# Sorted attention: the first group of 512 tokens in two halves of 256, with the second group's gathers moved behind both

## Chip, cores and metric

The kernel runs on one core of one Trainium2 chip. The metric is device time in microseconds (us), the median of several executions. A profile is one further execution with the hardware profiler on; times "at 1345" are us from the start of its span.

## What is computed

A block of two layers on 16 x 256 tokens of width 512, all in float32. The part that matters here is the second attention, after a mixture of experts:

```python
x = x + _L0_ffn_ref(_layernorm(x), ...)             # experts and shared network
x = x + _L1_xattn_ref(_layernorm(x), ctx, seg_id)   # the attention below
x = x + _L1_ffn_ref(_layernorm(x), ...)
...
q_c = q @ W_dq                                      # 512 -> 192
q_nope = q_c @ W_uq                                 # 16 heads of 128
q_rope = _rope(q_c @ W_qr)                          # 16 heads of 64
scores = (q_nope . k_nope + q_rope . k_rope) * scale
good = (k_ids <= seg) & (k_ids >= seg - 8)          # at most nine keys for a query
attn = softmax(where(good, scores, -1e30))
out = (attn @ v) @ W_o
```

## The kernel before

The program is laid out in stages: convolution with the shared network, experts (`routed`), the attention over sorted tokens (`attention_sorted`), the last network (`ffn`). An instruction scheduler places the instructions of each engine in a fixed order when the program is built, roughly in the order in which the code asks for them; every engine then works through its own queue in order. `tc.issue_after(i)` makes the instructions under it stand behind instruction `i`.

In `attention_sorted` the 4096 tokens have been sorted by the key they look at. They are worked on in 32 tiles of 128 tokens (`T`), four tiles to a group (`g`, 512 tokens, `T4 = 4`, `N = 512`). For a group:

- `fetch(T)` gathers, by indirect DMAs that GpSimd issues (line 1870), a tile's rows of x (`xt`) and its rope rows (`rr`); `fetch_routed` gathers, in two such DMAs, the experts' rows (`ygd`) that belong to it, into four buffers `g_yt`. `fetch_keys(T)` gathers a tile's windows of keys in four (`gw`). The x and rope rows of tiles 0 to 3 and the keys of tiles 0 to 2 are fetched in the stage before.
- `tokens` adds the gated experts' rows on VectorE (L1440), normalizes (`layernorm`: statistics L66 and L68 on VectorE, L70 and L71 on GpSimd, L72 on VectorE), and turns rope rows (L1448) and tokens (L99) on TensorE. `self.normed` is the last L71.
- `latents` makes q_c of the whole group (L1458, L1469).
- `heads(st, two)` makes four heads' queries for the whole group, and is called four times: matmuls L1482, L1485, L1489, L1493 into six of seven PSUM slots; ScalarE copies a swapped half (L1498), VectorE multiplies with the cosine (L1500), GpSimd with the sine (L1501) and adds (L1502); ScalarE stores the other queries (L1506). Results go to the big buffers `qn` and `qr`.
- For each tile `window` turns the keys (L1515, L1520) and makes masks, `scores` (L1543, L1549) needs the tile's part of `qn` and `qr`, `weigh` and `weights` are the softmax on VectorE and ScalarE, `values` is L1589, and `project` (L1605, 32 passes) adds to `xt` (L1610) and stores it.

The main loop (`for T in range(NT_ + 2)`) runs scores of tile T, values of T - 1, projection of T - 2, and puts the next group's fetches, `tokens`, `latents` and `heads` between them. Before the loop, group 0 goes through `tokens`, `latents` and `heads` with nothing else to do. The names `w`, `w_1`, `w_2`, `w_3` in the profile are large buffers that hold `qn`, `qr`, `ut`, `g_yt` and the like by turns.

Of the kernel before, what the change touches and what calls it, by code (L numbers as in the profile page):

```python
# [10 lines left out]
F32 = mybir.dt.float32  # L11
I32 = mybir.dt.int32
AF = mybir.ActivationFunctionType
ALU = mybir.AluOpType
# [4 lines left out]
P = 128  # L19
# [3 lines left out]
DC = D // P  # L23
# [11 lines left out]
CQ, WIN = 8, 32  # L35
# [7 lines left out]
class Kernel:  # L43
# [1329 lines left out]
    def attention_sorted(self, fetched, ygd, x3s, end_of_queries):  # L1373
        nc, tc = self.nc, self.tc
        wdq, m0, m1, wqr0, wqr1, nw = self.wdq, self.m0, self.m1, self.wqr0, self.wqr1, self.nw
        fetch, fetch_keys, xs, rrs, gws = fetched
        T4 = 4
        N = T4 * P
        HP = HEADS // 2
        NT_ = TOK // P  # L1380
        CH = N // CQ
        with ExitStack() as ctx:
# [5 lines left out]
            qn = self.e_w1.rearrange("p c x -> p (c x)").rearrange("p (c x) -> p c x", x=P)  # L1388
            qr = self.e_w2[:, 0 : CH * P // 2].rearrange("p (c x) -> p c x", x=P // 2)
# [14 lines left out]
            tp = pool("s_tok", 2)  # L1404
            small = pool("s_small", 4)
            kp = pool("s_win", 2)
            ap_ = pool("s_att", 2)
            ps_s = pool("s_ps_s", 1, space=PSUM)
            ps_m = pool("s_ps_m", 7, space=PSUM)
# [14 lines left out]
            def fetch_routed(st, t):  # L1424
                T = st["g"] * T4 + t
                st["y"].append([])
                for k in range(2):
                    yt = g_yt[rows_fetched[0] % 4]
                    rows_fetched[0] += 1
                    self.fetch_rows(yt, ygd, self.slot_s[:, k, T : T + 1], NT * P)  # L1430
                    st["y"][t].append(yt)
# [17 lines left out]
                nc.scalar.copy(st["rope"][:, :, toks], pt)  # L1449
                self.transposed(st["xT"][:, :, toks], xh, ps_m, "m")  # L1450

            def latents(st):
                lo, hi = slice(0, QC - P), slice(QC - P, P)
                pq = ps_m.tile([P, N], F32, tag="m", name="pq1")
                half = DC // 2
                for c in range(half):
                    for r, k in ((lo, c), (hi, half + c)):
                        nc.tensor.matmul(  # L1458
                            pq[r, :], wdq[:, k, P + r.start : P + r.stop], st["xT"][:, k, :],
                            start=(c == 0), stop=(c == half - 1), skip_group_check=True,  # L1460
                        )
                other = tp.tile([P, N], F32, tag="xh", name="other")
                for to, of in ((lo, hi), (hi, lo)):
                    nc.scalar.copy(other[to, :], pq[of, :])
                st["q1"] = g_q["q1"]
                nc.vector.tensor_tensor(st["q1"], other, pq, ALU.add)
                pq = ps_m.tile([P, N], F32, tag="m", name="pq")
                for c in range(DC):
                    nc.tensor.matmul(pq, wdq[:, c, 0:P], st["xT"][:, c, :], start=(c == 0), stop=(c == DC - 1))  # L1469
                st["q0"] = g_q["q0"]  # L1470
                nc.scalar.copy(st["q0"], pq)

            def heads(st, two):

                q0, q1 = st["q0"], st["q1"]
                pairs = (2 * two, 2 * two + 1)
                lo, hi = slice(0, QC - P), slice(QC - P, P)
                both = (lo, hi)
                pqr = [ps_m.tile([P, N], F32, tag="m", name="pqr") for hp in pairs]
                pqn = [[ps_m.tile([P, N], F32, tag="m", name="pqn") for i in range(2)] for hp in pairs]  # L1480
                for k, hp in enumerate(pairs):
                    nc.tensor.matmul(pqr[k], wqr0[:, hp * P : (hp + 1) * P], q0, start=True, stop=False)  # L1482
                for k, hp in enumerate(pairs):
                    for i in range(2):
                        nc.tensor.matmul(pqn[k][i], m0[:, 2 * hp + i, :], q0, start=True, stop=False)  # L1485

                for k in range(2):
                    rr = both[k]
                    nc.tensor.matmul(pqr[k], wqr1[rr, two, :], q1[rr, :], start=False, stop=True)  # L1489
                for k, hp in enumerate(pairs):  # L1490
                    for i in range(2):
                        rr = both[i]
                        nc.tensor.matmul(pqn[k][i], m1[rr, hp, :], q1[rr, :], start=False, stop=True)  # L1493
                by_chunk = lambda t: t.rearrange("p (c q) -> p c q", q=CQ)
                for k, hp in enumerate(pairs):
                    sw = ap_.tile([P, N], F32, tag="sw", name="sw", bufs=3)
                    for i in range(2):
                        nc.scalar.copy(sw[both[i], :], pqr[k][both[1 - i], :])  # L1498
                    to = qr[:, :, hp * CQ : (hp + 1) * CQ]
                    nc.vector.tensor_tensor(to, by_chunk(pqr[k]), by_chunk(st["rope"][:, 0, :]), ALU.mult)  # L1500
                    nc.gpsimd.tensor_tensor(sw, sw, st["rope"][:, 1, :], ALU.mult)  # L1501
                    nc.gpsimd.tensor_tensor(to, to, by_chunk(sw), ALU.add)  # L1502
                for k, hp in enumerate(pairs):
                    for i in range(2):
                        c0 = i * P // 2 + hp * CQ
                        nc.scalar.copy(qn[:, :, c0 : c0 + CQ], by_chunk(pqn[k][i]))  # L1506

            wins, last_at = {}, [None]

# [103 lines left out]
            new = lambda g: {"g": g, "y": []}  # L1613
            NG = NT_ // T4
            state = {0: new(0)}
            for t in range(T4):
                fetch_routed(state[0], t)
                tokens(state[0], t)
            first = self.normed
            latents(state[0])  # L1620
            window(0)
            for two in range(HP // 2):
                heads(state[0], two)
            ats, uts = {}, {}
            for T in range(NT_ + 2):
                g, t = T // T4, T % T4
                if T < NT_:
                    if 3 <= T + 2 < NT_:
                        fetch_keys(T + 2)
                    s = scores(state[g], T)  # L1630
                    e = weigh(T, s)
                    nxt = state.setdefault(g + 1, new(g + 1)) if g + 1 < NG else None
                    if nxt is not None and t < 2:
                        with tc.issue_after(first):
                            fetch((g + 1) * T4 + 2 * t)
                            fetch_routed(nxt, 2 * t)
                    if nxt is not None and t == 3:
                        latents(nxt)
                if 1 <= T <= NT_:
                    uts[T - 1] = values(T - 1, ats.pop(T - 1))  # L1640
                if T < NT_:
                    ats[T] = weights(e)
                    if T + 1 < NT_:
                        window(T + 1)
                    if nxt is not None and t == 3:
                        for two in range(HP // 2):
                            heads(nxt, two)
                if T >= 2:
                    project(state[(T - 2) // T4], T - 2, uts.pop(T - 2))
                if T >= NT_:  # L1650

                    if T == NT_:
                        end_of_queries()
                    which = T - NT_
                    xT = self.e_w2[:, which * DC * N : (which + 1) * DC * N].rearrange("p (c x) -> p c x", c=DC)
                    for k in range(T4):
                        xt = ap_.tile([P, N], F32, tag="sw", name="xt", bufs=3)
                        nc.sync.dma_start(xt, x3s[which][k * P : (k + 1) * P, :])
                        xh = tp.tile([P, D], F32, tag="xh", name="xh")
                        self.layernorm(xh, xt, small)  # L1660
                        self.transposed(xT[:, :, k * P : (k + 1) * P], xh, ps_m, "m")
                if T < NT_ and nxt is not None:
                    if t == 0:
                        with tc.issue_after(first):
                            fetch((g + 1) * T4 + 1)
                            fetch_routed(nxt, 1)
                    for k in ((0,), (1,), (2, 3), ())[t]:
                        tokens(nxt, k)
                    if t == 1:
                        with tc.issue_after(first):  # L1670
                            fetch((g + 1) * T4 + 3)
                            fetch_routed(nxt, 3)
            with tc.issue_after(last_at[0]):
# [363 lines left out]
```

## Time and profile before

| | us |
|---|---|
| median of three runs | 3091.67 (3091.25 to 3092.88) |
| the profiled execution's own time | 3093.04 |
| its span, first to last instruction | 3091.3 |
| TensorE busy in it | 3003.2 |
| mean granted TensorE clock | 0.989 |
| experts end, attention's first gather issued | 1298.3 |
| first matmul of latents, group 0 | 1320.3 |
| first projection (L1605) | 1398.6 |
| first matmul of latents, group 1 | 1415.6 |

A row of a timeline is: start, duration, engine, line, operation, output and input, count, and in brackets how long the engine was idle before it and who released it. A matmul in float32 shows as two passes, so that x8 is four instructions. In the chain of waits, a row is start, duration, engine, what.

### The profile page before, as it was taken

The page shows a single profiled execution, that of the slowest core. Times are in us where ns is not written, and L with a number is a line of the kernel's source. Part 1 is how long each engine was busy: PE and PEld are TensorE (multiplying, and loading weights), DVE is VectorE, ACT ScalarE, POOL GpSimd, SP SyncE. Part 2 cuts the span into 40 slices and gives each one's busy share as a digit, 9 for nine tenths or more (in the row PEclk, how much of TensorE's full clock was granted, in tenths as well). Part 3 has the DMA queues.
Part 4 walks back from the last instruction along what each step waited for, and adds up shares of the span by engine and source line. Part 5 has one row for each costly group of instructions (what it writes and reads, how often), then busy time and mean ns, then how long its engine had stood idle before and what let it go on. Part 6 is the DMA issues. An engine that isn't in the chain of part 4 may idle for free.

```text
span 3091.3 us, 34415 instructions
## 1 busy us (share of the span) xinstructions
PE 3003.2 (97%) x12713; PEld 1520.9 (49%) x12713; DVE 1438.2 (47%) x2675; ACT 652.8 (21%) x1213; POOL 910.9 (29%) x1216
## 2 busy tenths in 40 slices
PE   7999999999999999879999999999999999999998
PEld 4444444544545666534554554554444444444443
DVE  6877777677664444432433433433433232222222
ACT  1111111111111111134334333323111111111110
POOL 2233233232225000165545545544110300301201
PEclk9999999999999999989999999999999999999999
DMA  4232211211216643321311211211220100100100
GB/s 118 69 104 87 62 60 56 70 57 55 61 41 205 178 154 127 117 64 40 89 49 48 83 57 51 72 49 57 74 102 27 55 14 14 55 11 8 48 0 28
DMA packets 124720, 209.85 MB, mean 68 GB/s; under 512 B 33864, under 2 KB 53736, under 8 KB 123904
## 3 DMA queue, kind: packets, MB, share of 16 engines
q1 hardware_dynamic: 96256, 125.63, 13.7%
q0 software_dynamic: 28288, 81.92, 8.3%
q8 instruction: 104, 1.70, 0.2%
q14 instruction: 72, 0.59, 0.1%
HBM read 140.12 MB, written 67.37 MB: 67 GB/s over the span
## 4 chain that ended last, share of the span: by engine, by line
PE 86%; DVE 6%; issue 3%; POOL 2%; DMA 1%; SPq 0%; ACT 0%; POOLq 0%; DVEq 0%; ACTq 0%
PE y L292 15%; PE po L1830 14%; PE ph L1772 12%; PE po L1605 11%; PE pog L914 4%; PE phg L895 4%; PE pqn L1485 3%; PE pout L503 3%; PE ph L490 3%; PE pqr L1482 2%; PE pt L99 2%; PE pqn L1493 2%; DVE oT L304 1%; DVE pr L297 1%; PE pqr L1489 1%
## 5 line engine op out<-in xcount | busy, mean ns | idle before, releaser
L292 PE MATMUL y<-kv,ut 128*128 128x512 f32 x1280 | 563.1, 595 | 0.6 <-DVE pr L297 0.6
L1605 PE MATMUL po<-nw,w 128*128 128x512 f32 x1024 | 445.7, 594 | 0.0
L1830 PE MATMUL po<-p,ht 128*128 128x512 f32 x1024 | 445.3, 593 | 0.0
L292 PEld LDWEIGHTS y<-kv,ut 128*128 128x128 f32 x1280 | 243.3, 192 | 296.6 <-issue 287.1
L1605 PEld LDWEIGHTS po<-nw,w 128*128 128x128 f32 x1024 | 192.5, 190 | 234.7 <-issue 229.2
L1830 PEld LDWEIGHTS po<-p,ht 128*128 128x128 f32 x1024 | 193.1, 191 | 233.3 <-issue 231.5
L1772 PE MATMUL ph<-w,w 128*128 128x512 f32 x640 | 281.3, 593 | 0.2 <-ACT w L100 0.2
L297 DVE TENSOR_TENSOR pr<-y,cT 128x512 f32<-128x512 f32 x256 | 174.5, 682 | 148.2 <-PE y L292 148.2
L1834 DVE TENSOR_TENSOR res<-res,po 128x512 f32<-128x512 f32 x128 | 87.7, 685 | 314.4 <-PE po L1830 314.4
L1772 PEld LDWEIGHTS ph<-w,w 128*128 128x128 f32 x640 | 121.8, 190 | 152.8 <-issue 152.3
L304 DVE TENSOR_REDUCE oT<-pr 128x64 f32<-128x512 f32 x256 | 175.6, 686 | 8.8
L274 DVE TENSOR_TENSOR kv<-pvt,cT 128x512 f32<-128x512 f32 x256 | 174.0, 680 | 0.0
L1870 POOL DMA_INDIRECT gw<-kvd,keys_of x128 | 133.5, 1043 | 60.4 <-issue 36.3
L267 POOL TENSOR_TENSOR xt<-xt,sk 128x512 f32<-128x512 f32 x32 | 40.7, 1272 | 348.7 <-DVE sk L266 308.2
L1500 DVE TENSOR_TENSOR w<-pqr,w 128x512 f32<-128x512 f32 x64 | 44.2, 691 | 203.5 <-ACT sw L1498 203.5
L895 PE MATMUL phg<-w,xTg 128*128 x568 | 134.6, 380 | 0.5 <-DVE xTg L885 0.3
L914 PE MATMUL pog<-w,hT 128*128 x284 | 133.7, 593 | 0.0
L490 PE MATMUL ph<-xT,w_s 128*128 128x512 f32 x256 | 118.2, 607 | 0.0
L1772 PE MATMUL ph<-xT,w 128*128 128x512 f32 x256 | 116.4, 593 | 0.0
L1485 PE MATMUL pqn<-w,m 128*128 128x512 f32 x256 | 116.0, 597 | 0.0
L1786 ACT ACTIVATE ht<-ht,p1b 128x512 f32<-128x512 f32 x96 | 69.3, 722 | 213.7 <-DVE ht L1791 213.7
L503 PE MATMUL pout<-w_s,ht 128*128 128x512 f32 x256 | 113.6, 593 | 0.0
(290 smaller groups left out, 3750.2 us busy)
## 6 DMA issues: line engine op xcount, KB each, us to landing
xg<-xgd SPq DMA_DIRECT2D x71, 256.0 KB, 2.7
ygd<-y SPq DMA_DIRECT2D x71, 256.0 KB, 2.0
xt<-in_x_dram SPq DMA_DIRECT2D x32, 256.0 KB, 3.7
ct<-in_ctx_dram SPq DMA_DIRECT2D x32, 256.0 KB, 3.3
ut<-in_kt_dram SPq DMA_DIRECT2D x32, 256.0 KB, 2.7
w<-in_w_dram SPq DMA_DIRECT2D x8, 1024.0 KB, 5.5
x1d<-xt SPq DMA_DIRECT2D x32, 256.0 KB, 2.9
x3s<-xt POOLq DMA_DIRECT2D x32, 256.0 KB, 2.6
```

The source lines that it names most:

```text
L274: nc.vector.tensor_tensor(c["kv"][half][:, mc, :].rearrange("p (b j i) -> p b j i", i=NH, j=NH), c["vt"][:, mc, cols].rearrange("p (b i) - ...
L292: c["conv"] = nc.tensor.matmul(y, ut[:, (lc - mc) * P : (lc - mc + 1) * P], kv[:, mc, :], start=(mc == 0), stop=(mc == lc),).ins
L297: nc.vector.tensor_tensor(pr, y.rearrange("p (b j i) -> p b j i", i=NH, j=NH), cT[:, lc, cols].rearrange("p (b i) -> p b i", i=NH) .unsque ...
L304: nc.vector.tensor_reduce(c["oT"][:, lc, cols].rearrange("p (b j) -> p b j", j=NH), pr, AX.X, ALU.add)
L490: nc.tensor.matmul(ph, w["sw1"][:, c, f * P : (f + 1) * P], xT[:, c, :], start=(c == 0), stop=(c == DC - 1),)
L503: nc.tensor.matmul(po, st["ht"][f][:, tok], w["sw2"][:, f, :], start=(f == 0), stop=(f == NC_ - 1))
L895: nc.tensor.matmul(ph, xT[:, c, :], w1[:, c, bass.ds(e * EH, EH)], start=(c == 0), stop=(c == DC - 1))
L914: nc.tensor.matmul(po, hT[:, q, :], w2[:, bass.ds(e * (EH * D // P) + q * D, D)], start=(q == 0), stop=(q == EH // P - 1),)
L1485: nc.tensor.matmul(pqn[k][i], m0[:, 2 * hp + i, :], q0, start=True, stop=False)
L1605: nc.tensor.matmul(po, ut[:, n].rearrange("p a j q -> p (a j q)"), nw[:, 2 * hp + i, :], start=(n == 0), stop=(n == HEADS - 1),)
L1772: nc.tensor.matmul(ph, w[:, c, :], x[:, c, :], start=(start and c == 0), stop=(c == half - 1), skip_group_check=True,)
L1830: nc.tensor.matmul(po, ht[f, i // T4][:, toks], w2[:, f, :], start=(f == fs[0]), stop=(f == fs[-1]))
```

## The change

`latents` and `heads` take a range of tokens. Group 0 is split into `parts`, tiles 0 and 1, and tiles 2 and 3. Ahead of the loop now stand: gathers and `tokens` of tiles 0 and 1, `window(0)`, `latents` of the first half, the gathers of tiles 2 and 3 (behind the last norm of the first half), four half-wide `heads`, `tokens` of tiles 2 and 3, `latents` of the second half. The second half's four `heads` calls are made in the loop, two after the scores of tile 0, two after those of tile 1. Group 1's gathers, which were asked for from T = 0 on behind `first`, now come at T = 1 behind `turned`, the last GpSimd addition of the second half's rope, and at T = 2; its `tokens` come at T = 2 and T = 3. For later groups the order is as it was.

```diff
-            def latents(st):
+            def latents(st, toks=slice(0, N)):
...
-            def heads(st, two):
+            def heads(st, two, toks=slice(0, N)):
...
+                    turned = nc.gpsimd.tensor_tensor(to, to, by_chunk(sw), ALU.add).ins
...
-            for t in range(T4):
+
+            parts = (slice(0, N // 2), slice(N // 2, N))
+            TH = T4 // 2
+            for t in range(TH):
                 fetch_routed(state[0], t)
+            for t in range(TH):
                 tokens(state[0], t)
-            first = self.normed
-            latents(state[0])
             window(0)
+            latents(state[0], parts[0])
+            with tc.issue_after(self.normed):
+                for t in range(TH, T4):
+                    fetch_routed(state[0], t)
             for two in range(HP // 2):
-                heads(state[0], two)
+                heads(state[0], two, parts[0])
+            for t in range(TH, T4):
+                tokens(state[0], t)
+            latents(state[0], parts[1])
...
-                    if nxt is not None and t < 2:
-                        with tc.issue_after(first):
-                            fetch((g + 1) * T4 + 2 * t)
-                            fetch_routed(nxt, 2 * t)
+
+                    if nxt is not None:
+                        for k in () if g == 0 else ((0,), (2,), (), ())[t]:
+                            fetch((g + 1) * T4 + k)
+                            fetch_routed(nxt, k)
+                    if nxt is not None and g == 0 and t == 3:
+                        for k in range(TH, T4):
+                            tokens(nxt, k)
...
+                    if T < 2:
+                        for two in range(T * HP // 4, (T + 1) * HP // 4):
+                            turned = heads(state[0], two, parts[1])
...
                 if T < NT_ and nxt is not None:
-                    if t == 0:
-                        with tc.issue_after(first):
+                    if g == 0:
+                        if t == 1:
+                            with tc.issue_after(turned):
+                                for k in range(TH):
+                                    fetch(T4 + k)
+                                    fetch_routed(nxt, k)
+                        if t == 2:
+                            for k in range(TH):
+                                tokens(nxt, k)
+                                fetch(T4 + TH + k)
+                                fetch_routed(nxt, TH + k)
+                    else:
+                        if t == 0:
                             fetch((g + 1) * T4 + 1)
                             fetch_routed(nxt, 1)
-                    for k in ((0,), (1,), (2, 3), ())[t]:
-                        tokens(nxt, k)
-                    if t == 1:
-                        with tc.issue_after(first):
+                        for k in ((0,), (1,), (2, 3), ())[t]:
+                            tokens(nxt, k)
+                        if t == 1:
                             fetch((g + 1) * T4 + 3)
                             fetch_routed(nxt, 3)
```

More of the change, by code (lines that the diff above doesn't have):

```diff
@@ L1450, in tokens @@
                 self.transposed(st["xT"][:, :, toks], xh, ps_m, "m")
-            def latents(st):
+            def latents(st, toks=slice(0, N)):
+                n = toks.stop - toks.start
                 lo, hi = slice(0, QC - P), slice(QC - P, P)
-                pq = ps_m.tile([P, N], F32, tag="m", name="pq1")
+                pq = ps_m.tile([P, N], F32, tag="m", name="pq1")[:, 0:n]
                 half = DC // 2
@@ L1458, in latents @@
                         nc.tensor.matmul(
-                            pq[r, :], wdq[:, k, P + r.start : P + r.stop], st["xT"][:, k, :],
+                            pq[r, :], wdq[:, k, P + r.start : P + r.stop], st["xT"][:, k, toks],
                             start=(c == 0), stop=(c == half - 1), skip_group_check=True,
                         )
-                other = tp.tile([P, N], F32, tag="xh", name="other")
+                other = tp.tile([P, N], F32, tag="xh", name="other")[:, 0:n]
                 for to, of in ((lo, hi), (hi, lo)):
@@ L1465, in latents @@
                 st["q1"] = g_q["q1"]
-                nc.vector.tensor_tensor(st["q1"], other, pq, ALU.add)
-                pq = ps_m.tile([P, N], F32, tag="m", name="pq")
+                nc.vector.tensor_tensor(st["q1"][:, toks], other, pq, ALU.add)
+                pq = ps_m.tile([P, N], F32, tag="m", name="pq")[:, 0:n]
                 for c in range(DC):
-                    nc.tensor.matmul(pq, wdq[:, c, 0:P], st["xT"][:, c, :], start=(c == 0), stop=(c == DC - 1))
+                    nc.tensor.matmul(
+                        pq, wdq[:, c, 0:P], st["xT"][:, c, toks], start=(c == 0), stop=(c == DC - 1)
+                    )
                 st["q0"] = g_q["q0"]
-                nc.scalar.copy(st["q0"], pq)
-            def heads(st, two):
-                q0, q1 = st["q0"], st["q1"]
+                nc.scalar.copy(st["q0"][:, toks], pq)
+            def heads(st, two, toks=slice(0, N)):
+                n = toks.stop - toks.start
+                cs = slice(toks.start // CQ, toks.stop // CQ)
+                q0, q1 = st["q0"][:, toks], st["q1"][:, toks]
                 pairs = (2 * two, 2 * two + 1)
@@ L1478, in heads @@
                 both = (lo, hi)
-                pqr = [ps_m.tile([P, N], F32, tag="m", name="pqr") for hp in pairs]
-                pqn = [[ps_m.tile([P, N], F32, tag="m", name="pqn") for i in range(2)] for hp in pairs]
+                pqr = [ps_m.tile([P, N], F32, tag="m", name="pqr")[:, 0:n] for hp in pairs]
+                pqn = [[ps_m.tile([P, N], F32, tag="m", name="pqn")[:, 0:n] for i in range(2)] for hp in pairs]
                 for k, hp in enumerate(pairs):
@@ L1495, in heads @@
                 for k, hp in enumerate(pairs):
-                    sw = ap_.tile([P, N], F32, tag="sw", name="sw", bufs=3)
+                    sw = ap_.tile([P, N], F32, tag="sw", name="sw", bufs=3)[:, 0:n]
                     for i in range(2):
                         nc.scalar.copy(sw[both[i], :], pqr[k][both[1 - i], :])
[L1499 to L1502, printed above, removed]
+                    to = qr[:, cs, hp * CQ : (hp + 1) * CQ]
+                    nc.vector.tensor_tensor(to, by_chunk(pqr[k]), by_chunk(st["rope"][:, 0, toks]), ALU.mult)
+                    nc.gpsimd.tensor_tensor(sw, sw, st["rope"][:, 1, toks], ALU.mult)
+                    turned = nc.gpsimd.tensor_tensor(to, to, by_chunk(sw), ALU.add).ins
                 for k, hp in enumerate(pairs):
@@ L1505, in heads @@
                         c0 = i * P // 2 + hp * CQ
-                        nc.scalar.copy(qn[:, :, c0 : c0 + CQ], by_chunk(pqn[k][i]))
+                        nc.scalar.copy(qn[:, cs, c0 : c0 + CQ], by_chunk(pqn[k][i]))
+                return turned
             wins, last_at = {}, [None]
```

## The prediction

> **What bounds the kernel now.** I read the page first: its engine line for what is full, then a table by stage for where it isn't.
>
> ```profile
> PE 3003.2 (97%) x12713; PEld 1520.9 (49%) x12713; DVE 1438.2 (47%) x2675; ACT 652.8 (21%) x1213; POOL 910.9 (29%) x1216
> ```
>
> TensorE is the bound nearly everywhere; 88 us of the span are left to win from reordering. The table by stages (TensorE, weight load, VectorE, ScalarE, GpSimd busy, granted clock, DMA share, GB/s) covers the entry into the attention.
>
> ```profile
> 1298.30:1320.30 22.00, 6.15 (x24) 4.34 (x24) 10.93 (x20) 3.90 (x9) 14.97 (x18) 0.56 0.36 99
> 1320.30:1345.00 24.70, 17.69 (x51) 6.96 (x51) 11.63 (x21) 7.77 (x14) 19.95 (x24) 0.85 0.59 168
> 1345.00:1370.30 25.30, 25.30 (x70) 10.16 (x70) 3.58 (x6) 10.21 (x19) 17.46 (x17) 0.93 0.07 21
> 1370.30:1398.60 28.30, 18.16 (x391) 15.69 (x390) 14.68 (x31) 13.56 (x26) 11.58 (x11) 0.82 0.10 30
> 1415.60:1530.00 114.40, 114.09 (x817) 57.06 (x818) 44.17 (x85) 40.29 (x76) 62.22 (x62) 1.00 0.21 63
> ```
>
> Between 1298.3 and 1398.6 TensorE is idle 33 us, and its clock is 0.56 to 0.93; from 1398.6 it is full at clock 1.00. The waits of TensorE in 1298 to 1399 (total, times, longest) say for what:
>
> ```profile
> PE pt L99 <- DVE xh L72: 14.8, 4, 11.7
> PE pqr L1482 <- DVE w L1500: 7.0, 1, 7.0
> PE pu L1589 <- DVE at L1577: 6.5, 1, 6.5
> PE ps L1543 <- ACT w L1506: 2.1, 1, 2.1
> PE ps L1549 <- POOL w L1502: 1.6, 1, 1.6
> ```
>
> 14.8 is the norm of the first four tiles. The 7.0 is not rope arithmetic: VectorE's queue has the second group's gated sums (L1440) ahead of L1500, and these wait for gathers. GpSimd's timeline shows them:
>
> ```profile
> 1303.78 1.10 POOL L1870 DMA_INDIRECT w<-ygd,slot_s  x1 [0.30 <-issue]
> ...
> 1307.93 0.52 POOL L70 TENSOR_TENSOR ln_rs<-ln_mv,eps 128x1 f32<-128x1 f32 x1
> ...
> 1317.99 1.06 POOL L1870 DMA_INDIRECT xt<-x1d,order  x1 [0.17 <-issue]
> ...
> 1345.62 1.01 POOL L1870 DMA_INDIRECT w<-ygd,slot_s  x1 [0.30 <-DVE w L1500]
> ...
> 1347.48 1.25 POOL L1501 TENSOR_TENSOR sw<-sw,w 128x512 f32<-128x512 f32 x1
> ```
>
> Twenty gathers, 1.31 apart, fill 1318.0 to 1346.6; the rope (L1501) stands behind. In return, when the first projection ends at 1412.2, tiles 4 to 7 have long been ready.
>
> **The change, step by step.** In the built queues two gathers per tile for tiles 0 and 1 are issued, then their norms, then those of tiles 2 and 3; no gather of group two is ahead of a rope of group one. I follow the last releaser from step to step, with the old durations.
>
> 1. Entry. The gathered rows of tiles 0 and 1 land as before (sums L1440 at 1301.9, 1303.3, 1304.9, 1306.2). Tile 0's variance was ready at 1305.7, but L70 ran at 1307.9 behind gathers 5 to 7; now it runs at 1305.8. Tile 1's transpose comes at about 1310.2 (before 1312.9, and tile 3's at 1318.6). Two window transposes at half clock (1.1 each) and half latents (1.87 cold, then 1.73 warm: 8 passes) end at 1317.3; the first heads start at 1317.7 instead of 1328.8. Gathers 5 to 8 go at 1309.7 to 1313.6, tiles 2 and 3 are normed by 1321.5, and the first half-wide L1500 is due at 1321.6: just covered. Each us of delay there is a us of stall.
>
> 2. Heads by halves. From the chain, one whole call and a row with 256 columns:
>
> ```profile
> 1354.16 1.91 PE pqr L1482 x4
> 1356.07 3.43 PE pqn L1485 x8
> 1359.51 1.06 PE pqr L1489 x4
> 1360.57 1.72 PE pqn L1493 x8
> ...
> 1278.02 1.73 PE phg L895 x8
> ```
>
> A whole call is 8.12. L895 is 128x256: 8 passes in 1.73, half of L1485's 3.43, so a half call is 4.06 of matmuls. Its evictions: four 64x256 copies near 0.38 (a 128x256 copy, L1449, has 376 ns), four strided ones near 0.30 pipelined, two VectorE products near 0.42 (L899 128x256: 424 ns), four GpSimd ops near 0.73 (128x512 has 1.27, 128x1 0.2). With seven PSUM slots and six used, the next call's second pqn waits for the second product and the first for the first qn copy: about 0.2, so 4.26 a call. The 48 or so added instructions on ScalarE, VectorE and GpSimd lie beneath this (2.7, 0.8 and 2.9 a call against 4.26); at whole price they'd be 4.4, 1.4 and 5.1, and no longer hidden: that is rival (b). The 64-row passes at 256 columns have no row: half price from below, whole price (2.78 instead of 1.39) from above; I take half, since two such passes share the array and their loads too (pairs in 0.19). The Trainium skill, "TensorE: Matmul & The Clock Gate", section "Back-to-back issue gap", speaks against the change: a sustained matmul costs 131 ns at 512 columns and still 81 at 128. Interpolated (an estimate), 256 columns cost 98, or 0.75 of the whole, 6.05 a call. By the row eight half calls cost 32.5 in matmuls, as four whole ones do; by the rule 48.4. I go by the row: same kernel, same type.
>
> Four calls: 1317.7 + 4.06 + 3 x 4.26 = 1334.5 (before: 1370.3, where 7.0 of wait and a cold restart are inside).
>
> 3. First scores. After the last call the rope's tail was 5.0 (1370.3 to 1375.3); at half width 2.9, so 1337.4, with the transposes of tiles 2 and 3 (1.3) beneath. Half latents stand inside these scores: copies of xT until 1338.2, then 0.94 + 1.73, rest of the scores 1.3, window 1 1.1: 1343.3. Two calls (8.3), scores of tile 1 (1.8), values of tile 0 (1.1), window 2 (1.1): 1355.6. The 6.5 wait for the first softmax is gone: it lies under calls five and six (due 1353.4, ready 1349.9). Two more calls, their slots freed by ScalarE's value copies just in time: 8.5, 1364.1. The last rope, `turned`: +2.9 = 1367.0. Then scores 2 (1.6), the rest of values 1 and window 3 (2.0), and projection 0 at 1370.6 instead of 1398.6, ending at 1384.3.
>
> 4. What is late next. Group two's gathers are queued behind `turned` on GpSimd. Up to the last norm of tile 7 the built queue has 24 gathers (16 of tiles 4 to 7, four of window 4, four for group three) and four pairs L70/L71. Before, 20 gathers and three pairs took 28.6: 1.31 each, 0.8 a pair. So 24 x 1.31 + 4 x 0.8 = 34.6, to 1401.6. Waits for landed rows (3.5 to 4.0 after issue) fit inside: tile 7's last row lands at 1396.8. Norm 0.6, transpose 1.1, copy 0.6, hops 0.3: latents of group two at 1404.2. Before they were at 1415.6. TensorE alone would be there at 1384.3 + 4 x 0.66 + 1.9 = 1388.8, so 15 us of the 27 go back to the fetch, mainly as one wait of 8 for tile 5 (its L71 is behind window 4's gathers and others, 1394.7). VectorE now holds tile 4's sums and norm ahead of softmax 2 and stands at that norm until 1386; behind it wait the softmax of tile 2 (its values come after the latents, so 15 us of slack) and tile 5's statistics (ready 1388.5, wanted at 1392.6). The SyncE queue is not touched.
>
> 5. Clock. In this trace a 7.0 wait was followed by slow matmuls (L1482 x2 2.08 at 1345.0, against 0.96). If the latents run cold they cost 3.7 + 4.1 (as at 1320) against 5.5: +2.3. The same page, "The HAM clock gate", asks about 3.4 us of sustained work for full speed; scores 3 and the transposes are 4, with gaps. By that rule the loss may be 0; I take 2.3, since 1311 to 1320, a like mix, stayed slow.
>
> From the second latents on, TensorE's queue is the old one in the same order and is full in the stage table; group three's rows wait for stores of projections 0 to 3, which move along. Sum: 11.4 - 2.3 = 9.1 earlier. The profiled execution took 3093.04 with a span of 3091.3: that becomes 3083.9; the median 3091.67 becomes 3082.5.
>
> **Rivals.** (a) TensorE alone sets the end (26.8 earlier: 3065). For it: 33 us of idle exist. Against: GpSimd issues in order, and 34.6 of gathers stand between. 4%. (b) Half-wide steps keep more than half their price. Place: the eight calls before `turned`. It decides from 9.1/8, that is 1.15 more a call (5.4). By the page's 98 ns: 8 x 2.0 + 2.7 for latents = 18.7, so 9.6 later, 3101. For it: no row for the 64-row passes. Against: L895. 9%. (c) Gathers dearer than 1.31: their means run to 1.13 + 0.31 for rows of ygd, single ones to 1.5, landing to 5.9. 24 x 0.2 + 2 to 4 of latency eat 7 to 9: about 3090. For it: loads with several waits in one queue. Against: the twenty gathers measured together. 17%. (d) The forecast, 70%: 3082.5, with 3077 to 3088 by the entry (1.5), calls (2.5), gathers (2) and clock (2.3).
>
> **How the numbers follow.** 0.2%, about what a measurement of this kernel can tell from no change, is 6.2 us. Of (d) some 63 lie below 3085.5, 7 above; (a) adds 4, the gathers' case little: faster 0.68. Slower is (b), with 2 for what I don't see: 0.11. The rest, 0.21. The range reaches from 3076 to 3092: it leaves out (a), (b) and a little of both tails.
>
> **What would show it.** Right: first heads near 1318, first projection near 1371, no wait of TensorE for the rope product (L1505 in the changed file) above 1 us, a wait of about 8 for xh at tile 5, latents of group two near 1404, then no new idle. Wrong: half calls above 5 us; `turned` after 1372; gathers after it spaced over 1.5; or latents before 1395, which would mean a shorter queue than I counted.

## The result and the profile after

The changed kernel takes 3085.60 us (median of 20 runs, 3083.94 to 3090.62) against 3094.95 (3091.25 to 3099.52, 20 runs of the kernel before beside it): ratio 0.9974, 95% interval 0.9968 to 0.9981. On the 3091.67 of the prediction that is 3083.6. The profiled execution took 3089.02 with a span of 3087.2. (Group one is `g = 0` in the code, group two `g = 1`.)

The place at which the attention begins moves between executions, by work that the change doesn't touch: the first gather goes at 1298.32 in the trace before, at 1300.56 after, and between 1296.43 and 1300.78 in the traces below. So I count from the first gather, or shift a time so that this gather stands at 1298.3 ("in before's time"). The twenty times of the changed kernel stand in two clusters, eight near 3089 and twelve near 3085; its two traces (3089.02, and 3084.26 in e8) are one of each, and 3.5 of the 4.7 between them lie ahead of the first gather.

The table by stage for the entry (columns as before):

```profile
1318.87:1337.14 18.27, 18.14 (x97) 12.64 (x97) 5.42 (x12) 8.68 (x26) 10.53 (x16) 1.00 0.01 2
...
1346.25:1371.60 25.35, 23.82 (x248) 17.23 (x246) 14.74 (x31) 18.43 (x45) 16.29 (x20) 1.00 0.09 22
...
1389.10:1409.94 20.84, 7.82 (x122) 5.96 (x120) 11.27 (x24) 3.64 (x8) 17.44 (x22) 0.72 0.49 138
1409.94:1418.00 8.06, 8.06 (x16) 2.56 (x16) 3.94 (x10) 1.79 (x3) 5.17 (x6) 0.67 0.42 130
```

The four half calls (first row) and the stage with the other four (second) are nearly full, at clock 1.00. Part of what was lost has only moved. Up to the latents of group two TensorE is idle for 25 us instead of 33: 9.8 ahead of the first row, 2.5 from there to the last rope, and 13.0 behind the first projection (third row). And the latents run at clock 0.67 (fourth row). The waits of TensorE from 1300 to 1420:

```profile
PE pt L99 <- DVE xh L72: 21.2, 5, 8.2
PE ps L1555 <- POOL w L1507: 1.4, 2, 0.7
...
```

The waits of 7.0 and 6.5 are gone; the norms' wait grew from 14.8 to 21.2. GpSimd's timeline says what the norms wait for:

```profile
1370.86 0.72 POOL L1507 TENSOR_TENSOR w<-w,sw 128x256 f32<-128x256 f32 x1
1371.72 1.04 POOL L1902 DMA_INDIRECT xt<-x1d,order  x1
...
1407.06 0.56 POOL L71 TENSOR_TENSOR ln_rs<-ln_rs,mhalf 128x1 f32<-128x1 f32 x1
```

From the last rope to tile 7's norm, 24 gathers follow each other: 35.9 us. TensorE's timeline beside it:

```profile
1401.08 1.09 PE L99 MATMUL pt<-ident,xh 128*128 128x128 f32 x4 [7.96 <-DVE xh L72]
...
1409.94 2.83 PE L1459 MATMUL pq<-w,w_dq 128*64 128x512 f32 x6 [0.68 <-ACT w L100]
```

Tile 5 waits 7.96, and the latents of group two begin 109.4 after the first gather; before it was 117.2 (from 1298.32 to 1415.50 in the timeline). They end only 5.2 earlier, since they run cold (at clock 0.67 they take 8.06 us instead of 5.5), and from the first gather to the end of the span 6.3 are won (1786.6 against 1793.0).

### The profile page after: what moved, and what is told of

It is laid out like the page before. It is cut to its first block, busy times and chain, and to the rows that moved or that the text cites. A ratio compares the mean times of both kernels' runs of the same rounds, so it can differ in the third digit from the quotient of the medians.

```text
span 3087.2 us, 34716 instructions
## 1 busy us (share of the span) xinstructions
PE 3006.9 (97%) x12825; PEld 1530.4 (50%) x12825; DVE 1440.7 (47%) x2684; ACT 658.0 (21%) x1248; POOL 912.5 (30%) x1232
## 4 chain that ended last, share of the span: by engine, by line
PE 84%; DVE 6%; issue 5%; POOL 3%; DMA 1%; ACT 0%; SPq 0%; POOLq 0%; DVEq 0%; ACTq 0%
PE y L292 15%; PE po L1862 14%; PE ph L1804 12%; PE po L1611 8%; PE phg L895 4%; PE pog L914 4%; PE pout L503 4%; PE pqn L1490 4%; PE ph L490 3%; PE pqr L1487 2%; PE pqn L1498 2%; PE pt L99 2%; DVE oT L304 1%; PE pqr L1494 1%; DVE pr L297 1%
## 5 line engine op out<-in xcount | busy, mean ns | idle before, releaser
L1505 DVE TENSOR_TENSOR w<-pqr,w 128x512 f32<-128x512 f32 (+1 forms) x72 | 45.5, 632 | 201.9 <-ACT sw L1503 189.1
L895 PE MATMUL phg<-w,xTg 128*128 x568 | 134.6, 380 | 1.3 <-issue 0.7
L490 PE MATMUL ph<-xT,w_s 128*128 128x512 f32 x256 | 117.2, 602 | 0.0
L1490 PE MATMUL pqn<-w,m 128*128 128x512 f32 (+1 forms) x288 | 116.5, 546 | 0.2 <-ACT kn L1523 0.2
```

What stands on the lines that cost most here:

```text
L490: nc.tensor.matmul(ph, w["sw1"][:, c, f * P : (f + 1) * P], xT[:, c, :], start=(c == 0), stop=(c == DC - 1),)
L895: nc.tensor.matmul(ph, xT[:, c, :], w1[:, c, bass.ds(e * EH, EH)], start=(c == 0), stop=(c == DC - 1))
```

## The experiments

Theory A is that of the prediction: GpSimd's one queue, in order, sets when group two can start; where its gathers stand decides who waits. The rivals: B, the halves alone make the gain; C, the deferral alone; D, the place of the transposes alone. All ratios are to the kernel before, run beside it. The last column is the time from the first gather to the latents of group two.

| run | change | ratio, 95% interval | us |
|---|---|---|---|
| before | | 1 | 117.2 |
| after | | 0.9974, 0.9968 to 0.9981 | 109.4 |
| e1 | halves alone | 0.9996, 0.9988 to 1.0004 | 118.5 |
| e2 | gathers behind the ropes alone | 1.0008, 1.0002 to 1.0015 | 119.9 |
| e3 | after, 8 of 24 gathers later | 0.9979, 0.9973 to 0.9986 | 103.1 |
| e4 | after, 16 matmuls in the hole | 1.0011, 1.0002 to 1.0019 | 119.6 |
| e5 | e3, and tile 8's sums later | 0.9934, 0.9921 to 0.9948 | 103.0 |
| e6 | e5, six gathers in a gap | 0.9941, 0.9928 to 0.9955 | 103.1 |
| e7 | after, tile 8's sums later | 0.9971, 0.9960 to 0.9982 | 109.8 |
| e8 | after again | 0.9976, 0.9968 to 0.9985 | 109.6 |
| e9 | after without halves | 1.0011, 1.0002 to 1.0019 | 120.4 |
| e10 | e5 without halves | 0.9999, 0.9990 to 1.0007 | 120.4 |
| e11 | e5, four gathers in the gap, tile 4's sums later | 0.9925, 0.9911 to 0.9938 | 98.3 |

**The two parts alone.** e1 keeps the halves and puts group two's gathers back:

```diff
-                    if nxt is not None:
-                        for k in () if g == 0 else ((0,), (2,), (), ())[t]:
-                            fetch((g + 1) * T4 + k)
-                            fetch_routed(nxt, k)
...
+                    if nxt is not None and t < 2:
+                        with tc.issue_after(first):
+                            fetch((g + 1) * T4 + 2 * t)
+                            fetch_routed(nxt, 2 * t)
```

> The halves alone: group one's heads in two halves as in the changed kernel, but group two's gathers where they were before, behind the norms of tiles 2 and 3. In its built GpSimd queue 20 gathers stand among the first half's ropes. Theory A (GpSimd's in-order queue sets the entry; where its gathers stand only decides who waits): the ropes of the first half come some 18 us late, so the scores of tile 0 start near 1355 instead of 1337, projection 0 ends near 1403, no wait for tile 5, latents of group two near 1405: about 3084, ratio to before 0.995 to 0.999, no better than the changed kernel. Theory B (the halves make the gain, the deferral only gives some of it back): TensorE keeps the entry, latents near 1393, about 3070, ratio 0.993 or less. Theory C (the deferral makes the gain, halves none): 3092 or more, ratio 1.000 or above.

3092.82 against 3093.41. The first heads start 12.5 us earlier, and the waits of TensorE (1290 to 1425; total, times, longest) take it back:

```profile
PE pqr L1487 <- DVE w L1505: 13.7, 3, 6.8
PE ps L1555 <- POOL w L1507: 6.2, 2, 5.3
```

Two waits of over 6 for a rope product and one of 5.3 for a rope, since both stand behind gathers. The first scores' ropes came at 1360 in before's time, A had 1355; and from there to the end of projection 0 TensorE needs 53 us, 5 more than I had counted, so even A's 3084 was 9 too low. B falls; the number is the one that C had named.

e2 keeps whole heads and only puts the gathers behind the last rope:

```diff
-                        nc.gpsimd.tensor_tensor(to, to, by_chunk(sw), ALU.add)
+                        turned = nc.gpsimd.tensor_tensor(to, to, by_chunk(sw), ALU.add).ins
...
-                heads(state[0], two)
+                first = heads(state[0], two)
```

> The deferral alone: whole-width heads as before, with group two's gathers behind the last rope of group one. Theory A (GpSimd's queue): the wait of 7.0 for the first product between the first two heads calls goes, with about 1 us of cold matmuls behind it; last rope near 1367 instead of 1375.3, gathers behind it for some 35, last norm near 1402, latents of group two near 1405 to 1408 against 1415.5: about 3085, ratio 0.996 to 0.999, the same as the changed kernel, which would mean that the halves give nothing beyond it. Theory B (the halves make the gain): no gain, 3092 to 3100, ratio 1.000 or above. Theory C (deferral makes the gain): 3085, as in A.

3096.58 against 3093.41: no gain, against A and C both, and the number is B's. So e1 and e2 each speak for a theory that the other refutes. The wait of 7.0 is gone as expected and the scores of tile 0 start 9.6 us earlier, but TensorE's queue still has tile 4's transposes ahead of the values of tile 0, and they now come late:

```profile
1382.88 1.12 PE L99 MATMUL pt<-ident,xh 128*128 128x128 f32 x4 [7.12 <-DVE xh L72]
```

With a wait of 2.7 and one of 2.8 for a softmax behind tile 4's sums and norm on VectorE, all of it is given back before projection 0. I had followed only GpSimd's queue.

e9 asks whether that place is all (D): whole heads, with everything of group two where the changed kernel has it.

```diff
-            for t in range(TH):
+            for t in range(T4):
                 fetch_routed(state[0], t)
-            for t in range(TH):
                 tokens(state[0], t)
...
-                heads(state[0], two, parts[0])
+                turned = heads(state[0], two)
...
-                    if T < 2:
-                        for two in range(T * HP // 4, (T + 1) * HP // 4):
-                            turned = heads(state[0], two, parts[1])
```

> The changed kernel without its halves: group one's heads at whole width, all four calls ahead of the first scores, but the gathers and norms of group two in the places that the changed kernel gives them (the transposes of tiles 4 to 7 behind projection 0 on TensorE). This tells whether the deferral failed by itself only for where those transposes stood. Theory A (the halves are needed: with whole heads the first scores come only near 1362, so the first softmax is bare, some 10 us, and VectorE has tile 4's sums in the middle of it): values of tile 0 near 1383, projection 0 near 1394, latents of group two near 1412 against 1415.5: ratio 0.998 to 1.000. Theory D (the places alone do it; halves worth nothing, since the chain of gathers sets the end either way): latents near 1405, ratio 0.9965 to 0.998.

3096.23 against 3092.08. Now the softmax of tile 0 is bare:

```profile
1372.14 0.66 PE L1549 MATMUL ps<-w,kn 128*32 128x128 f32 x8 [4.08 <-DVE e L1565]
1381.49 2.09 PE L1595 MATMUL pu<-at,gw 32*128 32x128 f32 x32 [5.71 <-DVE at L1583]
```

Values of tile 0 come at 1382.5, as A had it, projection 0 at 1397.7 and the latents at 1418.7, 4 to 7 later than A had them. D falls. So neither part gives anything without the other. The halves put the first scores early and hide the softmaxes beneath the other four calls; the deferral keeps the ropes of the halves free.

**The chain of gathers.** e3 takes from the changed kernel's chain what tiles 4 to 7 don't need: the keys of tile 4 (and those of tile 5, fetched after them) and group three's rows stand behind tile 7's norm.

```diff
-                    if 3 <= T + 2 < NT_:
+                    if 3 <= T + 2 < NT_ and T not in (2, 3):
                         fetch_keys(T + 2)
...
-                            fetch((g + 1) * T4 + k)
-                            fetch_routed(nxt, k)
+                            with tc.issue_after(self.normed if t == 0 else last_norm):
+                                last_norm = self.normed if t == 0 else last_norm
+                                fetch((g + 1) * T4 + k)
+                                fetch_routed(nxt, k)
...
                             for k in range(TH, T4):
                                 tokens(nxt, k)
+                        with tc.issue_after(self.normed):
+                            fetch_keys(T4)
+                            fetch_keys(T4 + 1)
```

> The changed kernel, with the gathers that aren't needed for tiles 4 to 7 (four for window 4, four rows for group three) moved behind the last norm of tile 7: 16 gathers instead of 24 from the last rope to that norm. Theory A (the chain of gathers sets when group two's latents start): 8 x 1.31 = 10.5 less in the chain, latents near 1397 to 1399 instead of 1407.7 in before's time, the wait for tile 5 down from 8 to 3 or less, ratio to before 0.993 to 0.995, about 3075. If the cold clock and not the chain costs: 2 to 3 us at most, ratio 0.9965. If landing of rows or VectorE's sums set the end: nothing, ratio 0.9974 as the changed kernel; if the deferred gathers are then late for group three or window 4: slower than the changed kernel.

3087.73 against 3093.41: no faster than the changed kernel. And yet the chain did what A says: latents 103.1 after the first gather, 6.3 earlier than in the changed kernel, and warm (of the 10.5 taken from the chain 3.3 went into a new wait of GpSimd for VectorE's statistics). TensorE's timeline, and VectorE's, show what follows:

```profile
1419.30 1.12 PE L1526 MATMUL prw<-ident,gw 128*128 128x128 f32 x4 [11.47 <-DVE w L1467]
```

```profile
1416.43 0.75 DVE L1440 SCALAR_TENSOR_TENSOR xt<-w,routes,xt 128x512 f32<-128x512 f32 x1 [14.49 <-DMA xt<-x1d,order]
...
1418.56 0.68 DVE L1467 TENSOR_TENSOR w<-other,pq 128x512 f32<-128x512 f32 x1
```

The next window's transposes want the PSUM slot that the latents' addition (L1467) empties, and VectorE stands for 14.49 at the sum of tile 8 in front of it. Tile 8's row gather needs the buffer of tile 0, which is free once its row is stored (in the changed kernel this gather waits 0.79 for the store). VectorE has that row ready at 1397.95 (L1616), but GpSimd's timeline has:

```profile
1398.30 1.06 POOL L1908 DMA_INDIRECT gw<-kvd,keys_of  x1 [0.22 <-issue]
...
1409.12 0.62 POOL L1617 DMA_DIRECT2D x3s<-xt  x1
...
1412.71 1.00 POOL L1908 DMA_INDIRECT xt<-x1d,order  x1 [0.30 <-issue]
```

From 1398.30 on the eight moved gathers go one behind the other, and the store comes after them. Their 10.5 us have not gone; they have only moved to whoever stands behind the norm. A second floor, then, at about 1419, made by the place of the store in GpSimd's queue and by VectorE's order together. It is the third of the expectations (VectorE's sums), though with another tile's than I had meant. No run puts the store ahead of the moved gathers; e5 takes the other side, VectorE's order.

e5 is e3 with tile 8's sums moved behind group two's products:

```diff
+                    st["product"] = nc.vector.tensor_tensor(
...
                         for k in ((0,), (1,), (2, 3), ())[t]:
-                            tokens(nxt, k)
+                            with tc.issue_after(state[g]["product"]):
+                                tokens(nxt, k)
```

> The run before last (16 gathers instead of 24 ahead of the last norm of tile 7), and in addition tile 8's gated sums and norm moved behind group two's rope products in VectorE's queue. In that run the latents began early, but a wait of 11.5 followed, because VectorE stood at tile 8's sum (its rows' gather waits for the store of tile 0) ahead of the latents' addition L1467. Theory A (two floors in a row: the chain of gathers, then VectorE's order): the 11.5 goes, group two's heads follow the latents at once; latents near 1398 to 1400 in before's time and warm, 8 to 10 us earlier than in the changed kernel, less up to 3 for ropes behind gathers on GpSimd: 3076 to 3079, ratio 0.994 to 0.9955. If the rest of the queue can't be earlier whatever happens in the entry (stores of projections, rows of group three): 3086, ratio 0.9975.

3073.22 against 3094.44, somewhat more gain than A's 3076 to 3079. From the first gather, its latents end 9.0 earlier than those of the changed kernel (6.4 from the start, 2.5 since they are warm), and 2.7 more are won behind them. e7 has this edit alone:

> The changed kernel with only tile 8's gated sums and norm moved behind group two's rope products on VectorE. Theory A: in the changed kernel that order cost nothing yet (no wait of TensorE behind L1467, since the latents began as late as tile 8's rows came), so the time is that of the changed kernel, ratio 0.997 to 0.998. If VectorE's order is the only floor: faster, ratio 0.995 or less.

3085.84 against 3094.44, the time of the changed kernel. The second floor lay just beneath the first: either edit alone gives nothing (0.9979, 0.9971), both give 0.9934. e10 is e5 without the halves:

> The run before, with the gathers not needed for tiles 4 to 7 behind the last norm, and tile 8's sums behind group two's products (the two edits that together brought the changed kernel from 3086 to 3073). Theory A (with whole heads TensorE's own work, not the gathers, ends last in the entry): nothing more than the run before, ratio 0.998 to 1.000, 3088 to 3094; the difference to 3073 is then what the halves are worth once the queues are out of the way, 15 to 20 us. Theory D: near 3075, ratio 0.994.

3092.29 against 3092.08. With the same queues the halves are worth 0.9999 less 0.9934, some 20 us; the change as made collects 8 of them.

**The gap on GpSimd.** Between the ropes of the two halves GpSimd stood idle for 10.26. e6 is e5 with tile 4's rows fetched there:

```diff
             for t in range(TH, T4):
                 tokens(state[0], t)
+            state[1] = new(1)
+            with tc.issue_after(turned):
+                fetch(T4)
+                fetch_routed(state[1], 0)
```

> As the run before, and in addition tile 4's rows (and two for tile 5) fetched in the 10 us in which GpSimd stood idle between the ropes of the two halves: 10 gathers instead of 16 behind the last rope. Theory A (every gather behind the last rope costs its 1.3 until TensorE's own work, the end of projection 0 near 1389, is the later one): last norm near 1388, no wait for tile 5, latents near 1394 to 1396: another 4 to 5 us, about 3072, ratio 0.9925 to 0.994. If these gathers delay the second half's ropes in turn (the gap is not free, as with the halves alone): the last rope 3 to 8 us late, no gain over the run before or a loss.

3075.78 against 3094.44: no gain over e5; the other expectation came true. GpSimd's and TensorE's timelines:

```profile
1348.43 1.00 POOL L1915 DMA_INDIRECT w<-ygd,slot_s  x1 [2.25 <-DVE xt L1440]
```

```profile
1357.19 1.22 PE L1487 MATMUL pqr<-w,w_qr 128*128 128x256 f32 x2 [4.96 <-DVE w L1505]
```

Two gathers for tile 5 had come along and wait for the buffers of tile 4's; and VectorE stands at tile 4's sum (8.28), with the softmax of tile 0 and the product L1505 behind it. In e11 tile 4's and tile 5's sums stand behind the second half's last product, and only tile 4's four gathers fall into the gap:

```diff
                             for k in range(TH):
-                                tokens(nxt, k)
+                                with tc.issue_after(state[0]["product"]):
+                                    tokens(nxt, k)
```

> The fastest run so far (16 gathers behind the last rope, tile 8's sums later), with only tile 4's own four gathers in GpSimd's gap between the halves, and tile 4's sums and norm behind the second half's rope products on VectorE. The earlier attempt lost 5.0 in a wait for a product: two more gathers had to wait for the buffers of tile 4's rows, and VectorE stood at tile 4's sums. Theory A: the last rope is not late now, 12 gathers instead of 16 stand behind it, tile 4 is ready when projection 0 ends and tile 5 some 5 us earlier: the waits of 1.7 and 4.1 go, 4 to 6 us faster than the fastest so far: 3068, ratio 0.992. If any gather in the gap delays the ropes: the last rope 3 or more late, 3073 or more.

3070.69 against 3092.08, ratio 0.9925, about A's 0.992: faster than both kernels. Its interval overlaps that of e5; that it is the better of the two rests on the traces, where it is 3.6 shorter from the first gather to the end.

```profile
1393.87 0.66 PE L99 MATMUL pt<-ident,xh 128*128 128x128 f32 x4 [1.47 <-DVE xh L72]
```

Tiles 4 and 5 no longer wait, tile 6 waits 1.47, and the latents begin 98.3 after the first gather.

**The clock.** e4 puts 16 matmuls into TensorE's hole, so that it stays warm; nothing reads their output:

```diff
+                                if k == 1:
+                                    warm = ps_m.tile([P, N], F32, tag="m", name="warm")
+                                    for c in range(16):
+                                        nc.tensor.matmul(
+                                            warm, wdq[:, c % DC, 0:P], wdq[:, 0:2, :], start=True, stop=True
+                                        )
```

> The changed kernel with 16 matmuls of 128x512 more on TensorE, between the transposes of tiles 4 and 5, where it waited 8 us; their output is read by nobody. Sixteen of them last about 13.8 us at full clock (projection 0's 16 took 13.9), so they fill the hole and run over it by 5 to 6. Theory of the clock (cold latents cost 2.3 to 2.7): the latents then take 5.5 instead of 8.1, which pays back 2.6 of the 5 to 6 lost, and tile 5 to 7's transposes run without a wait (2 more back): net 0 to 2 us slower than the changed kernel, ratio 0.997 to 0.999. If the clock costs nothing there: 5 us slower, ratio about 0.999 to 1.000.

3098.24 against 3093.41, some 11 worse than the changed kernel, and useless for the clock: the built order of VectorE put tile 8's sums ahead of tile 7's norm (the second floor again, a wait of 8.05), so the latents came after a hole and ran cold. e8, the changed kernel again, tells more:

> The changed kernel itself once more beside these runs, for a second trace. All theories: ratio 0.9965 to 0.998. In its trace, entry, half calls of 4.6, last rope, 35.9 of gathers and latents near 1407 to 1408 (counted from a first gather at 1298.3) should come again; only the moment at which the entry starts may differ, by up to 3 us, from work before the attention that the change doesn't touch.

3086.22 against 3094.44, ratio 0.9976. The latents' first row in e8, and the same row in e7, after nearly the same waits:

```profile
1406.66 3.51 PE L1459 MATMUL pq<-w,w_dq 128*64 128x512 f32 x8 [0.68 <-ACT w L100]
```

```profile
1410.61 1.94 PE L1459 MATMUL pq<-w,w_dq 128*64 128x512 f32 x8 [0.67 <-ACT w L100]
```

Both stand behind a wait of 8 at tile 5 and one over 1 at tile 7 (e7 has 0.49 at tile 6 besides); one ran cold, the other warm.

## Why the prediction held, step by step

Times in before's time.

1. Entry: first heads at 1316.6, predicted 1317.7. Right, 1.1 to the good.
2. Heads by halves: the row of L895 was a good guide. A half call with no call just ahead of it takes 4.28 (the first, from 1318.87 to 1323.15) or 4.18 (the fifth), predicted 4.06. Eight passes of L1490 take 1.82, 228 ns each; eight of L1485 before, at 512 columns, took 3.52, 440 ns each. The 98 ns that I had interpolated (an estimate) from the Trainium skill ("TensorE: Matmul & The Clock Gate", "Back-to-back issue gap") made a half call 0.75 of a whole one, 6.05 us (0.75 x 8.12 is 6.09); measured are 0.51 to 0.53, so that rule does not hold for this kernel. Two sizes were off. The passes cost 0.2 a call more than half. And the stall for a slot in calls two to four is 0.35 to 0.42, not 0.2: L1487 takes 1.21 to 1.35 instead of 0.97, and L1490 another 0.1 in two calls. The view of L1487 over the four calls says what its engine (here the weight load) sat idle for, in us and times:

```profile
  DVE w L1505: 1.0, 3
```

VectorE's product in the call ahead empties the slot; the prediction had expected the stall at L1490. Together this is 18.27 for four calls instead of 16.84, 0.9 of it from the passes and 0.5 from the stalls. No run takes the stall away, so its price is read from the trace alone.

3. From the first scores to the last rope's end: 9.1 and 25.3, predicted 8.8 and 23.7. Of these four calls the fifth takes 4.18, the others 4.66 to 4.70. The last rope ends at 1369.3, predicted 1367.0.
4. What is late next: named rightly, 24 gathers, and the wait at tile 5 was 7.96 for 8. The chain took 35.9 for 34.6: 1.36 a gather instead of 1.31. Latents at 1407.7 instead of 1404.2: -1.1 + 1.4 + 0.3 + 1.6 + 1.3 = 3.5. e3 and e11 confirm the step: with 8 gathers fewer they start 6.3 earlier, with 12 fewer 11.1.
5. Clock: cold latents cost 2.5 (8.06 instead of 5.5), predicted 2.3. They were cold in both traces of the changed kernel, but warm in e7 after nearly the same waits, so 2.3 is not a fixed price, and that both traces paid it may be luck. By the same page's rule ("The HAM clock gate", about 3.4 us of sustained work) the loss could have been 0: that was so in e7, not in the other two.

Sum: 9.1 predicted. The latents' end came 5.2 earlier in the first trace, 5.9 in the second; 1.1 and 1.6 more were won behind them, of which 0.4 and 1.0 are short waits of TensorE for later tiles' norms and copies, and the ratio says 8.0 (3094.95 x 0.0026). The sum was 3 to 4 too high at the latents and 1 to 2 too low behind them, so a part of its closeness is luck. The profiled execution, forecast at 3083.9, took 3089.02: 2.2 of the difference is the later first gather, the rest the shortfall.

Rival (a) was priced at 3065 with a chance of 4%; its way is now visible: e11 gets most of it. The remark that 15 of 27 us go back to the fetch was nearly right: the first projection begins 25.4 us earlier and the latents 7.8, so 17.6 went back. What step 4 did not see is the second floor right behind it: the store of tile 0 behind the gathers, and VectorE's order with tile 8's sum ahead of L1467. In the changed kernel it costs nothing, so the forecast did not suffer; it is why e3 failed.

What stays open: what a call without the stall would be worth, and why the latents are cold in one execution and warm in the next.

## What to carry to other kernels

A queue that works in order is a budget: move gathers on it, and their 1.3 us each turn up at whoever stands next behind them, so write down for each engine what stands behind the moved work before counting a gain. Where two waits end within a few us of each other, removing either shows nothing (e3, e7; e1, e2); try the pair before dropping an idea. Only what the next step needs should stand ahead of it: eight gathers and one tile's sums in the wrong place hid 12 of the 20 us. And a thing moved out of the way stands in someone else's: ask what comes behind its new place (e3).

## What was not expected

An idle stretch of an engine is not free room: in e6, gathers in a gap of 10.26 made TensorE wait 4.96, through a buffer that was not free and through another engine's queue. And the latents after nearly the same pattern of waits took 5.5 us in one execution and 7.2 to 8.1 in two others.
